# A ConvNeXt block and a selective scan on one core: the first convolution's last 16 channels by halves of the images, the norm of the first half beside the second half's products, and the parameters loaded and used beside the convolution

## The chip, the cores and the metric

The kernel runs on one core of a Trainium2 chip. The time is the device time of one execution in microseconds, the median of several runs. Beside it there is one profiled execution, from which all durations are taken.

## What is computed

The input x has 32 images of 96 channels, 56 x 56, in float32. Two layers follow each other:

```python
# layer 0
h = conv_general_dilated(x, conv_w, padding 3, feature_group_count=C) + conv_b   # 7x7, depthwise
h = transpose(h, (0, 2, 3, 1))
mu, var = mean(h, axis=-1), var(h, axis=-1)              # over the 96 channels
h = (h - mu) * rsqrt(var + LN_EPS) * ln_g + ln_b
h = gelu(einsum('bhwc,cf->bhwf', h, w1) + b1)            # 96 -> 384, exact gelu
h = einsum('bhwf,fc->bhwc', h, w2) + b2                  # 384 -> 96
x = transpose(h, (0, 3, 1, 2)) * layer_scale + x
# layer 1
x = silu(conv_general_dilated(x, conv_w, padding 2, feature_group_count=C) + conv_b)  # 5x5, depthwise
# then a selective scan over the 3136 positions with N = 4 states per channel
```

The norm of a position needs all 96 channels of the convolution at that position: this is what separates the first convolution, which works channel by channel, from the MLP, which works on rows of the image with all channels.

## The kernel before, in words

There are four stages, and each hands its result to the next through a tensor in DRAM: conv1_d (first convolution), block_d (MLP), conv2_d (second convolution), and the output.

**Preparation (lines 86 to 228).** column() and across() and the lines to 131 load all parameters on SP's queue, ahead of the kernel taps of the first convolution (line 148). The taps are padded (pad, lines 149 to 156) and stored to taps1_d (157), from which the convolution reads them as Toeplitz matrices; the second convolution's taps go to taps2_d likewise (159 to 174). Lines 177 to 228 make the MLP's and the scan's weights: three groups of products (182, 190, 207), twelve copies from PSUM (185), and small operations on VectorE.

**First convolution (251 to 316).** The images are two halves (B2 = 2) of 16. The loop `for c in range(C)` takes one channel at a time: toeplitz() (234) loads the taps as two matrices into one of three buffers wts; two DMAs (272) load the channel's images of both halves into xt, 56 rows on the partitions each; POOL (281), VectorE (278) and ScalarE (279, 282) copy the odd and the even columns to xq, one of three buffers; eight products (286, each two records in the trace) go to a pair of PSUM banks; ScalarE evicts them with the bias (294) to ht, which POOL stores to conv1_d (298). The statistics run along: VectorE sums the difference to channel 0 (302, 303), ScalarE squares it (304), VectorE sums the squares (305). After the last channel lines 308 to 314 turn the sums of all 112 rows into reciprocal standard deviations, which SP stores to rstd_d (316).

**MLP (322 to 435).** The 112 rows (two halves of the images by 56) are taken in 28 groups of RB = 4, each in two half groups k. load_rows(n) issues on SP one load of r from rstd_d (345), three of h from conv1_d (350), one for each block of 32 channels with the four rows slowest, and twelve of x (355). normalise (362, VectorE), hidden (372 on TensorE, Gelu on ScalarE 382) and result (391 on TensorE, 402 on VectorE) follow. The tiles o, r, h, x and g are all in one pool, mlp, which lies on the memory that the first convolution's pools have left.

Then the second convolution and the scan, which are not changed.

**What sets the order.** A planner orders each engine's instructions ahead of time, by the order of the program and by when it expects operands to be ready; each engine then works through its own list in that order. pin (keep_in_program_order) puts an instruction behind the one written before it on its engine. normalise, hidden and the products of result are pinned, the loads of load_rows, the convolution and the preparation are not. A pool's `bufs` says how many tiles of one kind are there at once, and a new tile waits until the old one in its place has been used.

Of the kernel before, what the change touches and what calls it, by code (L numbers as in the profile page):

```python
# [38 lines left out]
EPS = 1e-9  # L39
RB = 4  # L40
# [6 lines left out]
def convnext_then_scan_kernel(  # L47
# [38 lines left out]
    def column(src, n, name):  # L86
        t = const.tile([n, 1], F32, name=name)
        nc.sync.dma_start(t, src.rearrange("(p o) -> p o", o=1))
        return t

    def across(src, parts, n, name):
        t = const.tile([parts, n], F32, name=name)
        nc.sync.dma_start(t, src.rearrange("(o n) -> o n", o=1).to_broadcast([parts, n]))
        return t
# [9 lines left out]

    c1b_t = across(c1b, ROWS, C, "c1b_t")
    c2b_t = across(c2b, 128, C, "c2b_t")
    g_t = column(ln_g, C, "g_t")
    lnb_t = column(ln_b, C, "lnb_t")
    b2_t = column(b2, C, "b2_t")
    ls_t = column(ls, C, "ls_t")  # L110
    ls_b = across(ls, 128, C, "ls_b")
    dtb_t = column(dtb, C, "dtb_t")
    ds_t = column(ds, C, "ds_t")
    w1_t = const.tile([C, F], F32, name="w1_t")
    nc.sync.dma_start(w1_t, w1)
    b1_t = const.tile([128, 3], F32, name="b1_t")
    nc.sync.dma_start(b1_t, b1.rearrange("(f p) -> p f", p=128))
    w2_t = const.tile([128, 3, C], F32, name="w2_t")
    nc.sync.dma_start(w2_t, w2.rearrange("(f p) c -> p f c", p=128))
    xp_t = const.tile([R, C], F32, name="xp_t")  # L120
    nc.sync.dma_start(xp_t, xp[:R, :])
    xpT_t = const.tile([C, R + 2 * N], F32, name="xpT_t")
    nc.sync.dma_start(xpT_t, xpT)
    dtwT_t = const.tile([R, C], F32, name="dtwT_t")
    nc.sync.dma_start(dtwT_t, dtwT)
    a_t = const.tile([128, NG], F32, name="a_t")
    for g in range(NG):
        nc.sync.dma_start(
            a_t[:, g : g + 1],
            bass.AP(alog.tensor, alog.offset + g * DG, [[1, DG], [C, N], [1, 1]]),  # L130
        )

    w1r_t = const.tile([128, C // CB, F], F32, name="w1r_t")
    b1p_t = const.tile([128, 3], F32, name="b1p_t")
    b2r_t = const.tile([128, C // CB], F32, name="b2r_t")
    wd_t = const.tile([C, C], F32, name="wd_t")
# [5 lines left out]
    with tc.tile_pool(name="prep", bufs=1) as prep, tc.tile_pool(  # L142
        name="prep_ps", bufs=1, space=PSUM
    ) as prep_ps:


        kt = prep.tile([C, K1, K1], F32, name="kt1")
        nc.sync.dma_start(kt, c1w.rearrange("c (i j) -> c i j", j=K1))
# [3 lines left out]
        for i in range(3):  # L152
            for t in range(P1):
                j = 2 * t + 1 - i
                if j in range(K1):
                    nc.vector.tensor_copy(pad[:, i, at : at + K1, t], kt[:, :, j])
        nc.sync.dma_start(taps1_d, pad.rearrange("c d p t -> c (d p t)"))

        kt = prep.tile([C, K2, K2], F32, name="kt2")
        nc.sync.dma_start(kt, c2w.rearrange("c (i j) -> c i j", j=K2))  # L160
        turned = prep.tile([C, K2, K2], F32, name="turned")
        for r in range(K2):
            nc.vector.tensor_copy(turned[:, r], kt[:, K2 - 1 - r])
        pad = prep.tile([C, QC, 2 * RW, QC * 2], F32, name="pad2")
        nc.vector.memset(pad, 0.0)
        for k in range(QC):
            for f in range(QC):
                for t in range(2):
                    j = 4 * t + (k if k < 2 else k - 4) - f + K2 // 2
                    if j in range(K2):  # L170
                        nc.vector.tensor_copy(
                            pad[:, k, RW - K2 : RW, f * 2 + t], turned[:, :, j]
                        )
        nc.sync.dma_start(taps2_d, pad)
# [76 lines left out]
    with tc.tile_pool(name="c1", bufs=3) as pool, tc.tile_pool(  # L251
# [4 lines left out]
        for t in wts + xqs:  # L256
            nc.vector.memset(t, 0.0)
# [544 lines left out]
```

## Time and profile before

| | |
|---|---|
| time, median of 3 runs | 3655.25 us (3648.51 to 3655.76) |
| profiled execution: its own time | 3655.9 us |
| profiled execution: span, first to last instruction | 3654.1 us |
| mean granted TensorE clock | 0.827 |
| busy: PE, VectorE (DVE), ScalarE (ACT), GpSimd (POOL) | 3060.6, 2655.5, 2341.0, 1950.5 us |
| first convolution: first product, last product ends | 27.9, 609.8 us |
| MLP: first product, last product ends | 644.3, 1496.0 us |
| second convolution: first product | 1506.5 us |

Lines of the profile name an engine, a line of the kernel, and what is written from what. PE is TensorE's products, PEld its weight loads, SPq the queue of SyncE, which issues DMAs. A bracket gives the idle time of the engine before the instruction and what ended it. Buffer numbers are left out of the names: ps is any ps tile, w_t is w1_t or w2_t. The share of DMA is the mean over the core's 16 DMA engines; the granted clock is a share of full speed.

### The profile page before, as it was taken

How to read it: one execution, taken by the hardware profiler on the slowest of the kernel's cores; microseconds unless marked ns; L12 is line 12 of the kernel's file. 1: busy time of each engine (PE TensorE's matmuls, PEld its weight loads, DVE VectorE, ACT ScalarE, POOL GpSimd, SP SyncE). 2: the span in 40 equal slices, each digit the busy share in tenths (PEclk: the TensorE clock that was granted, in tenths of full speed). 3: DMA queues.
4: the chain of work that ended last, by engine and by line, in shares of the span. 5: the costliest groups of instructions: out<-in, count | busy, mean ns of one | idle time of the engine just before them, and what ended most of it. 6: DMA issues, size and time to landing. Idle time of an engine off the chain costs nothing. (4 is left out here: it accounts for less than half of the span.)

```text
span 3654.1 us, 46458 instructions
## 1 busy us (share of the span) xinstructions
PE 3060.6 (84%) x17290; PEld 1286.4 (35%) x17290; DVE 2655.5 (73%) x1771; ACT 2341.0 (64%) x2133; POOL 1950.5 (53%) x1241
## 2 busy tenths in 40 slices
PE   7999996899999999899957777777777777777775
PEld 5777774333333333333312222222222222222221
DVE  5666665233333333599949999999999999999998
ACT  3555553333333333577858878888888888888884
POOL 2333332122222222100028999999999999999996
PEclk9999998899999999999966666666666666666666
DMA  5555553455555554699977778877877877878873
GB/s 153 166 167 167 168 168 107 149 162 160 163 163 162 162 160 125 169 281 281 288 232 264 259 253 281 276 257 267 276 260 267 281 245 275 274 244 277 281 258 108
DMA packets 302054, 790.70 MB, mean 216 GB/s; under 512 B 123012, under 2 KB 180164, under 8 KB 277156
## 3 DMA queue, kind: packets, MB, share of 16 engines
q1 hardware_dynamic: 259076, 669.31, 56.7%
q0 software_dynamic: 28416, 79.87, 7.3%
q10 hardware_dynamic: 14336, 38.54, 2.7%
q8 instruction: 137, 2.24, 0.3%
q14 instruction: 89, 0.73, 0.1%
HBM read 551.83 MB, written 235.74 MB: 216 GB/s over the span
## 5 line engine op out<-in xcount | busy, mean ns | idle before, releaser
L682 POOL TENSOR_TENSOR hs<-hs,ct 128x1568 f32<-128x1568 f32 x192 | 673.3, 3507 | 104.8 <-DVE hs L671 93.0
L664 DVE TENSOR_TENSOR_SCAN pv<-rep,pv 128x1568 f32<-128x1568 f32 x192 | 664.5, 3461 | 72.2 <-ACT rep L650 54.2
L654 POOL TENSOR_TENSOR rep<-rep,bt 128x1568 f32<-128x1568 f32 x192 | 674.9, 3515 | 14.6 <-DMA rep<-du_d 14.6
L382 ACT ACTIVATE g<-ph,b1p_t 128x896 f32<-128x896 f32 x336 | 320.5, 1005 | 511.8 <-PE ph L372 511.8
L402 DVE SCALAR_TENSOR_TENSOR o<-po,b2r_t,x 128x224 f32<-128x224 f32 x336 | 190.4, 608 | 572.4 <-PE po L391 572.4
L286 PE MATMUL ps<-xq,wt 120*112 120x448 f32 x1536 | 581.9, 540 | 14.1 <-POOL xq L281 14.1
L414 POOL DMA_DIRECT2D block_d<-o x336 | 183.7, 553 | 703.5 <-DVE o L402 621.3
L286 PEld LDWEIGHTS ps<-xq,wt 120*112 120x112 f32 x1536 | 429.4, 280 | 166.2 <-POOL xq L281 14.3
L372 PE MATMUL ph<-h,w1r_t 32*128 32x448 f32 x4032 | 440.3, 559 | 55.8 <-DVE h L362 54.4
L599 POOL TENSOR_TENSOR du<-du,xs 96x784 f32<-96x784 f32 x128 | 236.3, 1847 | 373.7 <-ACT du L593 373.7
L585 PE MATMUL pz<-xs,wd_t 96*96 96x392 f32 x512 | 277.3, 707 | 172.0 <-ACT du L593 139.1
L391 PE MATMUL po<-g,w_t 128*32 128x448 f32 x4032 | 413.1, 543 | 0.0
L695 PE MATMUL py<-hs,sel_t 128*32 128x392 f32 x1536 | 328.6, 685 | 68.5 <-POOL hs L682 68.5
L630 PE MATMUL pk<-bn,pick_t 8*128 8x392 f32 x1024 | 287.3, 682 | 98.4 <-ACT y L705 78.8
L667 DVE SCALAR_TENSOR_TENSOR pv<-pv,rep 128x1568 f32<-128x1568 f32 x192 | 345.6, 1800 | 21.1 <-POOL hs L682 1.4
L480 PE MATMUL ps<-xq,wt 128*32 128x448 f32 x3072 | 309.9, 548 | 39.3 <-DMA xq<-block_d 36.5
L671 DVE TENSOR_TENSOR_SCAN hs<-rep,carry_h,pv 128x1568 f32<-128x1568 f32 x96 | 334.0, 3479 | 10.4 <-DVE pv L667 0.5
L503 DVE COPY st<-yt 28x896 f32<-28x896 f32 x288 | 317.7, 1103 | 26.9 <-DMA conv_d<-st 13.2
L671 DVE TENSOR_TENSOR_SCAN hs<-rep,pv 128x1568 f32<-128x1568 f32 x96 | 328.4, 3421 | 10.3 <-DVE pv L667 0.9
L688 PE MATMUL py<-xs,dsm_t 96*96 96x392 f32 x512 | 308.6, 746 | 11.7 <-ACT bn L618 6.1
L648 ACT ACTIVATE rep<-rep,a_t 128x1568 f32<-128x1568 f32 x192 | 308.3, 1606 | 11.6 <-DMA rep<-du_d 11.2
L649 ACT ACTIVATE rep<-rep,lift_t 128x1568 f32<-128x1568 f32 x192 | 307.6, 1602 | 6.2
(85 smaller groups left out, 3155.4 us busy)
## 6 DMA issues: line engine op xcount, KB each, us to landing
rep<-du_d SPq DMA_DIRECT2D x192, 1568.0 KB
du_d<-du SPq DMA_DIRECT2D x128, 588.0 KB
xq<-block_d SPq DMA_DIRECT2D x192, 225.0 KB
block_d<-o POOLq DMA_DIRECT2D x336, 120.0 KB, 5.6
xt<-in_x_dram SPq DMA_DIRECT2D x192, 196.0 KB
h<-conv_d SPq DMA_DIRECT2D x84, 448.0 KB
x<-in_x_dram SPq DMA_DIRECT2D x336, 112.0 KB
conv_d<-st SPq DMA_DIRECT2D x96, 392.0 KB
```

Of the source, the lines that this page charges most:

```text
L286: nc.tensor.matmul(ps[:, j, :PQ].rearrange("p (i r) -> p i r", i=BI), lhsT=wv[:KR, t], rhs=xq[:KR, j, :, t : t + W2], start=(t == 0), stop ...
L372: pin(nc.tensor.matmul(phs[i // 2][:, i % 2, :HALF], lhsT=w1r_t[rows, d, f * 128 : (f + 1) * 128], rhs=hts[n, d][rows, s * HALF : (s + 1) ...
L382: nc.scalar.activation(gt, ph[:, :, :HALF], AF.Gelu, bias=b1p_t[:, f : f + 1], scale=1.0)
L391: pin(nc.tensor.matmul(po[CB * i : CB * i + CB, :HALF], lhsT=w2_t[:, f, CB * d : CB * d + CB], rhs=gts[n, s, f, i // 2][:, i % 2], start=( ...
L480: pin(nc.tensor.matmul(ps[RW * f : RW * f + RW, h, : B * QW].rearrange("p (b q) -> p b q", q=QW), lhsT=wv[:, f, t], rhs=xv[:, :, t : t + Q ...
L503: pin(copy(st[:, :, :, :, f], yt[RW * f : RW * f + QR].rearrange("p h (b q) -> p h b q", q=QW),))
L654: pin(nc.gpsimd.tensor_mul(ut, ut, bts[i // NG]))
L664: pin(nc.vector.tensor_tensor_scan(grown, da, zero, pv[:, last : last + 1] if q else 1.0 / EPS, ALU.mult, ALU.add))
L667: pin(nc.vector.scalar_tensor_tensor(run, in0=grown, scalar=1.0, in1=ut, op0=ALU.min, op1=ALU.mult))
L671: pin(nc.vector.tensor_tensor_scan(ht, da, run, carry_h[:, col : col + 1] if q else 0.0, ALU.mult, ALU.add))
L682: pin(nc.gpsimd.tensor_mul(ht, ht, cts[k]))
L695: pin(nc.tensor.matmul(py[g * DG : (g + 1) * DG, s, :BK], lhsT=sel_t, rhs=hss[k * NG + g][:, cols], start=False, stop=True, tile_position= ...
```

## The change

The parameters are loaded on ScalarE's queue, and SP begins with the taps and the images of two channels. The weights of the MLP and the scan and the second convolution's taps are made in 13 pieces (beside), one behind each job from the fourth on, and their products use the convolution's PSUM tiles. The convolution's loop runs over jobs: 80 channels with both halves of the images, then 16 channels with the first half alone, then the same 16 with the second half. Taps are loaded four jobs ahead into five buffers, images two jobs ahead. The norm is computed by halves of the images (finish_norm): the first after the second job of the second half (job 97), the second inside the MLP at k == 3. Its store goes from SP to POOL's queue. The MLP's pool is split in three: o and g (14 buffers instead of 15) lie below, on the convolution's memory, and r, h and x above them. Some memsets go from VectorE to POOL, among them those of o.

```diff
+APART = 16
...
-    def column(src, n, name):
-        t = const.tile([n, 1], F32, name=name)
-        nc.sync.dma_start(t, src.rearrange("(p o) -> p o", o=1))
-        return t
...
+    front = ctx.enter_context(ExitStack())
+    stats = front.enter_context(tc.tile_pool(name="stats", bufs=1))
+    first = stats.tile([ROWS, B2, HALF], F32, name="first")
+    acc1 = stats.tile([ROWS, B2, HALF], F32, name="acc1")
+    acc2 = stats.tile([ROWS, B2, HALF], F32, name="acc2")
+    sq = stats.tile([ROWS, B2, HALF], F32, name="sq")
+
+    def finish_norm(j):
+
+        a1, a2 = acc1[:, j], acc2[:, j]
+        nc.vector.tensor_mul(sq[:, j], a1, a1)
+        nc.vector.scalar_tensor_tensor(
+            a2, in0=sq[:, j], scalar=-1.0 / C, in1=a2, op0=ALU.mult, op1=ALU.add
+        )
+        nc.vector.tensor_scalar(a2, a2, 1.0 / C, 0.0, ALU.mult, ALU.max)
+        nc.scalar.activation(a2, a2, AF.Sqrt, bias=eps_t[:ROWS], scale=1.0)
+        nc.vector.reciprocal(a1, a2)
+        for s in range(2):
+            nc.gpsimd.dma_start(
+                rstd_d[j * H : (j + 1) * H, s * PQ : (s + 1) * PQ], a1[s * H : (s + 1) * H]
+            )
+
+    with tc.tile_pool(name="c1", bufs=3) as pool, tc.tile_pool(
+        name="c1k", bufs=1
+    ) as keep, tc.tile_pool(name="prep", bufs=1) as prep, tc.tile_pool(
+        name="c1_ps", bufs=4, space=PSUM
+    ) as psum:
+        wts = [keep.tile([128, 2, H * P1], F32, name=f"wt1_{i}") for i in range(5)]
+        xqs = [keep.tile([128, B2, BI, W2 + 3], F32, name=f"xq_{i}") for i in range(3)]
+        jobs = [(c, (0, B2)) for c in range(C - APART)]
+        jobs += [(c, (j, j + 1)) for j in range(B2) for c in range(C - APART, C)]
...
+        kt1 = prep.tile([C, K1, K1], F32, name="kt1")
+        nc.sync.dma_start(kt1, c1w.rearrange("c (i j) -> c i j", j=K1))
+        xts: dict = {}
+
+        def load_x(n):
+            c, js = jobs[n]
+            xts[n] = pool.tile([128, COLS], F32, name=f"xt1_{n}", tag="xt")
+            for j in range(*js):
+                nc.sync.dma_start(xts[n][MP * j : MP * j + H], x[c, j * H : (j + 1) * H])
+
+        for n in range(2):
+            load_x(n)
+
+        def column(src, n, name, pool=prep):
+            t = pool.tile([n, 1], F32, name=name)
+            nc.scalar.dma_start(t, src.rearrange("(p o) -> p o", o=1))
+            return t
...
+        c1b_t = across(c1b, ROWS, C, "c1b_t", const)
...
         nc.sync.dma_start(taps1_d, pad.rearrange("c d p t -> c (d p t)"))
+        for t in wts + xqs + [acc1, acc2]:
+            nc.vector.memset(t, 0.0)
+
+        c2b_t = across(c2b, 128, C, "c2b_t", const)
+        dtb_t = column(dtb, C, "dtb_t", const)
+        g_t = column(ln_g, C, "g_t")
...
+        w1_t = prep.tile([C, F], F32, name="w1_t")
+        nc.scalar.dma_start(w1_t, w1)
...
+        def bank(name):
+            return psum.tile([128, B2, 512], F32, name=name, tag="ps")
...
+        def first_weights():
+
+            cen = prep.tile([C, C], F32, name="cen")
+            nc.vector.tensor_scalar(cen, ident[:C, :C], -1.0 / C, None, ALU.add)
+            nc.vector.tensor_scalar(w1g, w1_t, g_t, None, ALU.mult)
+            held["w1"] = bank("ps_w1")[:, 0]
+            nc.tensor.matmul(held["w1"][:C, :F], lhsT=cen, rhs=w1g, start=True, stop=True)
+            ps = bank("ps_b1")[:, 0]
...
+        def first_rows(i):
+            for d in range(C // CB):
+                nc.vector.tensor_copy(
+                    w1r_t[CB * i : CB * i + CB, d, :], held["w1"][CB * d : CB * d + CB, :F]
+                )
...
+        beside = [first_weights] + [lambda i=i: first_rows(i) for i in range(RB)]
+        beside += [second_weights, scan_weights, scan_rows, turn_taps]
+        beside += [lambda k=k: second_taps(k) for k in range(QC)]
+
+        def taps_of(n):
+
+            c, wt = jobs[n][0], wts[n % len(wts)]
+            for s in range(2):
...
+                nc.sync.dma_start(wt[MP * s : MP * s + H], taps)
+
+        for n in range(4):
+            taps_of(n)
+        for n, (c, js) in enumerate(jobs):
+            if n + 4 < len(jobs):
+                taps_of(n + 4)
+            if n + 2 < len(jobs):
+                load_x(n + 2)
+
+            xq, xt = xqs[n % len(xqs)], xts.pop(n)
+            for j in range(*js):
                 xv = xt[MP * j : MP * j + H].rearrange("p (i r s) -> p s i r", i=BI, s=2)
...
+                copy = nc.vector.tensor_copy if j else nc.gpsimd.tensor_copy
+                copy(xq[:H, j, :, 2 : W2 + 2], xv[:, 1])
+                nc.scalar.copy(xq[MP:KR, j, :, 1 : W2 + 1], xv[:, 0])
...
+            half = slice(*js)
+            ht = pool.tile([ROWS, B2, HALF], F32, name=f"ht_{n}", tag="ht") if c else first
             nc.scalar.activation(
-                two(ht), ps[:, :, :PQ], AF.Identity, bias=c1b_t[:, c : c + 1], scale=1.0
+                ht[:, half], ps[:, half], AF.Identity, bias=c1b_t[:, c : c + 1], scale=1.0
             )
...
+                nc.vector.tensor_sub(dt[:, half], ht[:, half], first[:, half])
+                nc.vector.tensor_add(acc1[:, half], acc1[:, half], dt[:, half])
+                nc.scalar.activation(dt[:, half], dt[:, half], AF.Square)
+                nc.vector.tensor_add(acc2[:, half], acc2[:, half], dt[:, half])
+            if n >= 3 and beside:
+                beside.pop(0)()
+            if n == C + 1:
+                finish_norm(0)
...
-    with tc.tile_pool(name="mlp", bufs=2) as pool, tc.tile_pool(
+    with tc.tile_pool(name="mlp_ot", bufs=1) as pool_o, tc.tile_pool(
+        name="mlp_g", bufs=14
+    ) as pool_g, tc.tile_pool(name="mlp", bufs=2) as pool, tc.tile_pool(
...
         for t in ots:
-            nc.vector.memset(t, 0.0)
+            nc.gpsimd.memset(t, 0.0)
...
-                gt = pool.tile([128, 2, HALF], F32, name=f"g_{n}_{s}_{f}_{a}", tag="g", bufs=15)
+                gt = pool_g.tile([128, 2, HALF], F32, name=f"g_{n}_{s}_{f}_{a}", tag="g")
...
+            if k == 3:
+                finish_norm(1)
...
+    front.close()
```

## Prediction

> **What bounds the kernel now.** I read the span and clock first, then the busy shares by stretch, then the timeline and the waits around the two places that the change touches: the start and the seam between first convolution and MLP. By stretch (columns: stretch, its length, busy microseconds of PE, PEld, DVE, ACT, POOL with instruction counts, granted clock, DMA share, GB/s):
>
> ```profile
> 0.00:60.00 60.00, 35.70 (x88) 24.33 (x89) 34.75 (x103) 16.75 (x23) 10.16 (x24) 1.00 0.53 146
> 300.00:360.00 60.00, 60.00 (x161) 44.51 (x160) 36.67 (x40) 31.40 (x41) 18.59 (x30) 1.00 0.54 167
> 1620.00:3654.00 2034.00, 1540.40 (x6660) 506.85 (x6651) 1892.03 (x775) 1624.47 (x1347) 1586.88 (x608) 0.70 0.78 260
> ```
>
> The first convolution is bound by PE (60.00 of 60; DVE, ACT and POOL have room), the scan, which is not changed, by DVE. The waits of the first 60 us (columns: us in total, times, longest):
>
> ```profile
> POOL xq L281 <- DMA xt<-in_x_dram: 29.9, 3, 25.9
> ...
> PE ps L286 <- POOL xq L281: 14.1, 1, 14.1
> ```
>
> and of the seam, 600 to 660:
>
> ```profile
> PE ph L372 <- DVE h L362: 39.8, 3, 34.4
> ...
> DVE h L362 <- DMA h<-conv_d: 15.3, 3, 8.2
> ```
>
> At the start PE has nothing of the convolution until the images come; in the timeline its first product stands at 27.90. At the seam PE is idle for 34.4 us in one piece:
>
> ```profile
> 609.94 1.01 ACT L294 ACTIVATE ht<-ps,c1b_t 112x896 f32<-112x896 f32 x1 [1.73 <-PE ps L286]
> ...
> 619.59 5.75 DVE L314 RECIPROCAL acc<-acc 112x896 f32<-112x896 f32 x1 [2.45 <-ACT acc L313]
> 625.37 0.75 SPq L316 DMA_DIRECT2D rstd_d<-acc  x2
> 628.58 0.62 SPq L345 DMA_DIRECT2D r<-rstd_d  x1
> 628.85 0.86 DVE L335 MEMSET o<- 128x960 f32 x1 [3.50 <-DMA rstd_d<-acc]
> 629.25 3.16 SPq L350 DMA_DIRECT2D h<-conv_d  x3
> ...
> 642.97 1.09 DVE L362 TENSOR_TENSOR h<-h,r 128x896 f32<-128x896 f32 x1 [8.23 <-DMA h<-conv_d]
> 644.27 1.88 PE L372 MATMUL ph<-h,w1r_t 32*128 32x448 f32 x8 [34.42 <-DVE h L362]
> 647.48 1.09 DVE L362 TENSOR_TENSOR h<-h,r 128x896 f32<-128x896 f32 x1 [3.42 <-DMA h<-conv_d]
> 652.22 1.09 DVE L362 TENSOR_TENSOR h<-h,r 128x896 f32<-128x896 f32 x1 [3.64 <-DMA h<-conv_d]
> ```
>
> It is a chain: last statistics and norm (609.9 to 625.3), store and reload of the norm (to 628.6 and on), then three loads of h that land 4.5 us apart. Behind it PE restarts at half clock. The whole price: the MLP ends at 1496.0 (last L391 product); its normalisations recur every 29.98 us, so its 56 half groups need 56 x 14.99 = 839.5, and it starts in effect at 656.5. The convolution's products end at 609.8, so the seam costs **46.7 us**.
>
> Last, the order in which SP issues (end of the convolution):
>
> ```profile
> 575.46 0.76 SPq L272 DMA_DIRECT2D xt<-in_x_dram  x2
> 579.73 12.81 SPq L242 DMA_DIRECT2D wt<-taps_d  x6
> ```
>
> The last channel's images are issued ahead of the taps of three channels: a load that isn't pinned goes out as soon as it can, not in program order. And the first memset of o waits for the store of acc, a tile of the pool that its own pool lies on: a pool waits for what was beneath it.
>
> **What the Trainium skill says.** DMA: Bandwidth & Descriptors, section on why a DMA increments its semaphore by 16: a DMA runs on the largest number of engines up to 16 that divides the slowest dimension on both sides. The loads of r and h have four rows there, so 4 of 16; the trace agrees (DMA share 0.24 in 630 to 635, and 448 KB in 4.5 to 4.7 us). Same page, queues and rings: each queue's descriptors are taken in ring order, so an image load behind such loads waits on those four engines; the trace has the h loads one after another, but not yet such a mix. TensorE: Matmul & The Clock Gate, Part 1: an idle window of about 3.4 us halves the clock; the trace has 0.50 from 615 to 660 and 1.00 from 665. ScalarE: Activation LUTs, on the cost of a table load: about 1283 ns; the trace has 1.28 us.
>
> **The change, part by part.** The sum is made against the profiled execution, 3655.9 us (span 3654.1 and 1.8 around it); the median shown, 3655.25, is 0.65 lower.
>
> *Start.* SP's 21 parameter DMAs before the first kernel taps (0.47 us apart, so taps only at 10.45) go away; taps and two channels of images come first. Taps issued at 0.74 land about 2.5 us later (an issue to landing of 2.2 to 4.4 us is seen at 8.5 to 12.1 and 3.1 to 7.5), ten copies to pad take 0.83: 4.2. The store of the taps to its first reload took 20.77 - 17.11 = 3.7: 8.0. Reload, as image loads in before (24.28 to 27.22), 2.9 with its issue, two of them 0.38 apart: 11.3. ACT now issues 19 DMAs ahead of its first copies: 0.32 each (L706, its only DMA row) to 0.47 (SP's spacing) gives 6 to 9 us, then probably a table load of 1.28 and a copy of 0.59: 8.6 to 11.5. So 11.3 to 11.5, if nothing comes between. But the MLP's r, h and x tiles now sit in a pool beyond everything that the convolution uses, so the 36 x loads for which there are buffers (9 tiles of 4) depend on nothing and may float into SP's idle time here: 0.42 us each, from none to 36 x 0.42 = 15 us. I take three: **first product at 12.5**, a gain of 27.9 - 12.5 = **-15.4** (0 to -16.6).
>
> *Parameter work beside the products.* PE gets 2 + 6 + 2 records (L182, L190, L207: 3.66 us at the start, where the array was cold); warm, **+2.3** (1.8 to 3.7), now on the path. DVE gets about 14 us (12 copies L185 of 0.56, 20 of L171 of 0.08, the rest small) over 13 jobs, at most 1.7 in one; it is busy 36.67 of 60, 3.7 a channel of 6.03, so 2.3 are free: nothing, and without that cover up to 14. The weight tile holds one of four PSUM pairs for some jobs; eviction takes 1.01 us, so two would do. Memsets moved to POOL aren't in the trace there (128x128 takes 0.20, DVE 0.86 for 128x960): 0.9 to 1.5 each, six of them, not before the first result needs them: nothing, at worst a few us.
>
> *Halves.* 16 channels become 32 jobs of half the products, 3.01 us each: PE's sum is unchanged. Per job, taps are loaded anew: 2 x 98 + 196 KB in, 196 out, in 3.01 us, or 200 GB/s against 167 (share about 0.65). SP needs 3 issues, 1.2 us; DVE half of three 1.09 and a copy of 0.39, 2.1; ACT about 1.7; POOL at most 0.58 + 1.28. All fit in 3.01. Images are issued some 4.5 jobs ahead (575.46 against a first product at 603): 13.5 us of lead in halves, some 10 after landing and copy. Into this come the norm of half one (half of 1.09 + 1.09 + 0.63 + 1.04 + 5.75, a table load, so 6.1 us) and up to nine h loads and three r loads. The wait for Sqrt holds ACT's evictions and copies behind it, the store of the norm now holds POOL's convolution stores: each by some us, against three output buffers (9 us). Most h loads (channels below 64) can go out long before, where the lead is 27 us; three h and three r in the halves are 6 x 4.6 = 28 us of the four engines, not all at once. I take **+3** (0 to 46, see the rivals).
>
> *Seam.* Norm of half one is done some 25 us before the products end: job 97's statistics about 10 us into the second half of 48, then 6.1 + queueing and a store of 3.6. So r and h can be there. What is late next: DVE's tail of the last job, since the first normalisation is pinned behind it: eviction 0.57, two half operations 1.1, Square 0.5, one more 0.55, about 3.1; three normalisations of 1.09 make 6.4; the third block's products start there. In before that point (653.36) lay 3.1 ahead of the effective start; with 4 instead of 34 idle us I take 2.5: 9 us. If the last h load is behind stores or SP's last taps, 12 to 15. I take **12 instead of 46.7: -34.7** (9 to 24).
>
> *Second norm inside the MLP.* 4.4 us of DVE and up to two table loads (2.6), where PE is the limit (29.76 of 30.30) and ACT 11.4, DVE 10 of 30.3: hidden by three PSUM pairs, **+1** (0 to 4). 14 instead of 15 g tiles: twelve are live at most: 0.
>
> Sum: -15.4 + 2.3 + 3 - 34.7 + 1 = -43.8; 3655.9 - 43.8 = 3612.1, so **3612**.
>
> **Rivals.** (A) *The h loads wait for the last convolution store anyway* (one tensor, conv1_d, is written in all jobs). Then they go out at 0.6 + 3.6 = 4.2 after the products, land at 4.2 + 2.5 + 3 x 4.6 = 20.5, effective start 24: **3624**. For it: h waited in before. Against: in the scan, stores to du_d follow 0.05 us after loads of other parts of it, without waiting. (B) *The x loads float ahead of the taps*: 15 us at the start, **3627**. For it: 575.46 above. Against: SP is idle there for some us only. (C) *Slower*: nine h and three r loads pile up on four engines in front of the second half's images. Each takes 4.6 us alone; if convolution traffic stretches them to 7, 84 us less 10 of lead is a stall of 74, and the seam then takes 9: 3655.9 - 15.4 + 2.3 + 74 + 9 - 46.7 + 1 = **3680**. It decides from a stall of 46.7 - 9 + 15.4 - 2.3 - 1 = 50, that is from 5 us a load ((50 + 10) / 12) with all twelve together. Against: most can go out earlier, and r only late.
>
> **How the numbers follow.** Forecast 0.58, its own range 3600 to 3620 (best: start at 11.3, no stall, seam 9); A 0.18; B 0.12; a stall as in C, but only of some 40 us, near 3650, 0.04; C 0.08. The range of 8 in 10 takes in A and B and one short stall: 3600 to 3638. About 0.2%, 7.3 us, is what a measurement of this kernel can tell from no change. Faster 0.88 (forecast, A, B), same 0.04, slower 0.08.
>
> **What would show it.** Right: the first convolution product at 11 to 14; the stretch of products with no gap except around the parameters; r and h issued on SP before the last products; the third normalisation within 12 us of the last product; clock at 0.5 for no more than some us; the scan unchanged in length. Wrong: the first product beyond 18 (B); h issued after the last store (A); PE waiting for xq or xt in the halves, with DMA share near a quarter (C).

## The result, and the profile after it

| | before | after |
|---|---|---|
| median of 4 runs each, us | 3654.06 | **3616.1** |
| lowest to highest | 3648.51 to 3655.76 | 3614.36 to 3618.94 |
| profiled execution: time / span | 3655.9 / 3654.1 | 3618.94 / 3617.1 |
| mean granted clock there | 0.827 | 0.831 |

The ratio after / before is **0.9899**, with a 95% interval of 0.9885 to 0.9912: about 38 us, or 1.0%, faster. The prediction was 3612.

The same view by stretch as before the change (stretch, its length, busy us of PE, PEld, DVE, ACT, POOL, granted clock, DMA share, GB/s), the last row being the second convolution and the scan, whose code is the same:

```profile
0.00:60.00 60.00, 42.11 (x110) 29.79 (x111) 40.28 (x106) 22.11 (x30) 15.30 (x32) 1.00 0.62 179
300.00:360.00 60.00, 60.00 (x160) 44.51 (x160) 36.65 (x40) 31.59 (x40) 18.38 (x30) 1.00 0.54 168
...
573.00:583.00 10.00, 7.65 (x21) 5.25 (x20) 3.04 (x6) 2.29 (x4) 1.65 (x4) 1.00 0.47 151
...
604.00:614.00 10.00, 2.15 (x14) 0.95 (x16) 8.41 (x13) 2.77 (x5) 2.85 (x6) 0.79 0.38 148
...
1584.00:3617.00 2033.00, 1533.68 (x6648) 507.00 (x6640) 1890.48 (x774) 1624.57 (x1346) 1586.11 (x608) 0.70 0.79 260
```

PE does 6.4 us more in the first 60; the middle of the convolution and the scan are as they were. Of the seam, where PE stood for 34.42 us in before, 7.85 us are left in the row from 604. New is a hole in the row from 573: PE 7.65 of 10 in the middle of the half jobs.

The first product of the convolution in the kernel before:

```profile
27.90 32.36 PE L286 MATMUL ps<-xq,wt 120*112 120x448 f32 x78 [14.10 <-POOL xq L281]
```

Timeline of PE in the kernel after: the first products, the parameter products among them, the end of the convolution and the first product of the MLP.

```profile
17.89 26.72 PE L334 MATMUL ps<-xq,wt 120*112 120x448 f32 x64 [17.89 <-DMA wt<-taps_d]
44.45 0.81 PE L247 MATMUL ps_w<-w1g,cen 96*96 96x384 f32 x2
...
579.70 24.77 PE L334 MATMUL ps<-xq,wt 120*112 120x448 f32 x64 [2.35 <-ACT xq L329]
612.32 5.38 PE L421 MATMUL ph<-h,w1r_t 32*128 32x448 f32 x28 [7.85 <-DVE h L411]
```

The convolution now starts at 17.89 instead of 27.90, has one gap of 2.35 us, ends at 604.47 (579.70 + 24.77), and the MLP's first product follows after 7.85 us instead of 34.42.

To add the parts up, I use the prediction's own measure: the MLP needs 56 x 14.99 = 839.5 us, so its **effective start** is its last product (1457.46 here) less 839.5, which is 618.0; the **seam** is that less the end of the convolution, 618.0 - 604.5 = 13.5. Five terms then make up the span:

| term, us | before | after | difference | predicted |
|---|---|---|---|---|
| first product of the convolution | 27.9 | 17.9 | -10.0 | -15.4 |
| first to last product of the convolution | 582.0 | 586.6 | +4.6 | +2.3 + 3 |
| seam | 46.7 | 13.5 | -33.2 | -34.7 |
| last product of the MLP to the first of the second convolution | 10.5 | 12.0 | +1.5 | 0 |
| from there to the end | 2147.6 | 2147.6 | 0.0 | 0 |

(The MLP's 839.5 is a constant of this measure; the term +1 for the second norm inside it is in the seam, and none of it is seen.) The differences sum to -37.1, the spans differ by -37.0; the terms predicted sum to -43.8. The 4 us between the predicted 3612 and the median of 3616.1 flatter the prediction a little: the execution that the terms are taken from took 3618.94.

One warning on reading the experiments: the last term is the same code in all kernels, but from run to run it came out between 2137.3 and 2147.6; that it is equal before and after is chance. Differences of less than some 10 us between two versions are therefore read from the terms ahead of it, not from the totals, and where an expected total was missed the text says so but rests nothing on it.

### The profile page after: what moved, and what is told of

It is laid out like the page before. It is cut to its first block, busy times and chain, and to the rows that moved or that the text cites. A ratio compares the mean times of both kernels' runs of the same rounds, so it can differ in the third digit from the quotient of the medians.

```text
span 3617.1 us, 46656 instructions
## 1 busy us (share of the span) xinstructions
PE 3051.3 (84%) x17290; PEld 1285.1 (36%) x17290; DVE 2659.5 (74%) x1816; ACT 2347.6 (65%) x2166; POOL 1973.9 (55%) x1286
## 5 line engine op out<-in xcount | busy, mean ns | idle before, releaser
L334 PE MATMUL ps<-xq,wt 120*112 120x448 f32 x1536 | 582.9, 540 | 20.2 <-DMA wt<-taps_d 17.9
L334 PEld LDWEIGHTS ps<-xq,wt 120*112 120x112 f32 x1536 | 428.7, 280 | 172.7 <-issue 20.2
L701 ACT ACTIVATE rep<-rep,a_t 128x1568 f32<-128x1568 f32 x192 | 308.4, 1606 | 13.5 <-DMA rep<-du_d 13.1
L702 ACT ACTIVATE rep<-rep,lift_t 128x1568 f32<-128x1568 f32 x192 | 307.7, 1602 | 6.2
L703 ACT ACTIVATE rep<-rep,lift_t 128x1568 f32<-128x1568 f32 x192 | 307.6, 1602 | 6.3
```

What stands on the lines that cost most here:

```text
L334: nc.tensor.matmul(ps[:, j].rearrange("p (i r) -> p i r", i=BI), lhsT=wv[:KR, t], rhs=xq[:KR, j, :, t : t + W2], start=(t == 0), stop=(t = ...
```

## The experiments

None of these kernels leaves out any of the computation. All are edits of the kernel after, unless said. "Ratio" is to the kernel before, run on the same chip beside it. The terms come from each kernel's own trace:

| kernel | first product | convolution | seam | second convolution begins at | median | ratio, 95% |
|---|---|---|---|---|---|---|
| before | 27.9 | 582.0 | 46.7 | 1506.5 | 3654.06 | 1 |
| after | 17.9 | 586.6 | 13.5 | 1469.5 | 3616.1 | 0.9899 [0.9885, 0.9912] |
| no_halves | 17.8 | 584.0 | 51.9 | 1503.2 | 3647.89 | 0.9991 [0.9985, 0.9998] |
| no_halves_r_first | 17.4 | 584.2 | 30.5 | 1481.4 | 3626.49 | 0.9928 [0.9915, 0.9942] |
| one_pool | 18.0 | 582.8 | 34.0 | 1487.0 | 3626.96 | 0.9929 [0.9915, 0.9944] |
| params_late | 12.1 | 585.9 | 13.7 | 1463.6 | 3606.48 | 0.9879 [0.9862, 0.9895] |
| norm_free | 18.2 | 590.2 | 13.7 | 1473.9 | 3617.38 | 0.9906 [0.9892, 0.9921] |
| h_by_rows | 17.2 | 583.4 | 10.6 | 1464.0 | 3605.58 | 0.9875 [0.9861, 0.9888] |
| square_late | 17.0 | 597.8 | 10.5 | 1477.1 | 3620.82 | 0.9918 [0.9904, 0.9931] |
| half_8 | 17.1 | 583.7 | 17.7 | 1468.0 | 3614.67 | 0.9898 [0.9884, 0.9911] |
| late_rows | 12.1 | 584.1 | 10.6 | 1459.1 | 3603.81 | 0.9866 [0.9853, 0.988] |
| late_rows_square | 11.9 | 583.7 | 10.5 | 1458.7 | 3601.43 | 0.9862 [0.9848, 0.9875] |
| late_rows_8 | 11.8 | 584.3 | 10.3 | 1456.0 | **3596.9** | 0.9849 [0.9836, 0.9863] |

### What the seam is made of: the halves, the pools, the order

**no_halves** keeps the new start and the new pools, and takes the halves back:

```diff
-APART = 16
+APART = 0
...
-            if n == C + 1:
-                finish_norm(0)
+        for j in range(B2):
+            finish_norm(j)
...
-            if k == 3:
-                finish_norm(1)
```

> All 96 channels with both halves of the images, both norms computed after the last channel; early parameters, split pools and everything else as in the changed kernel. Theory (the seam shrinks for two reasons of about the same size: the norm of one half is ready before the products end, and the loads of h and x no longer wait for the convolution's memory): the norm is on the path again, some 12 us to the first half's reciprocal, 3 to store it, 7 for r to land, while h is already there; effective start of the MLP 26 to 30 us after the last product (46.7 before, 13.5 changed), no stall in the halves; time 3627 to 3632. Rival 1 (the early loads alone do it): seam 14 to 18, time 3616. Rival 2 (the norm's halves alone do it): seam 44 to 47, time 3645 to 3649.

Measured: 3647.89, ratio 0.9991. The 10 us won at the start are there; 5.2 are lost again at the seam, 51.9 instead of 46.7, and 2.0 in the convolution, which now holds the parameter products. The theory's time was missed by 16 us. The time is the one that rival 2 gave, but not for its reason: the seam is longer than in any of the three. Its trace at the seam, DVE, PE and SP (for SP, the second number is how long it took over the issues):

```profile
607.32 19.11 SPq L399 DMA_DIRECT2D h<-conv_d  x7
626.56 24.75 SPq L394 DMA_DIRECT2D r<-rstd_d  x4
...
647.69 3.09 DVE L411 TENSOR_TENSOR h<-h,r 128x896 f32<-128x896 f32 x3 [30.39 <-DMA r<-rstd_d]
...
648.93 6.20 PE L421 MATMUL ph<-h,w1r_t 32*128 32x448 f32 x28 [47.09 <-DVE h L411]
```

With pools of their own, the h tiles have room at once, and the loads of h need only the convolution's stores: seven of them, 448 KB each on four DMA engines, go out at 607.32, ahead of r, which needs the norm and is issued at 626.56. All three normalisations then wait for that one r until 647.69; from 626 to 646 the DMA share is 0.25, four engines of 16. Here an early load was an advantage only for the load that was needed first.

**no_halves_r_first** tests that reading. It is no_halves with the h loads from the second group on held in program order, so that they can't pass r:

```diff
-                nc.sync.dma_start(ht, rows_of(conv1_d, row, d))
+                ins = nc.sync.dma_start(ht, rows_of(conv1_d, row, d))
+                if n:
+                    pin(ins)
```

> The kernel without halves (both norms after the last channel), with the h loads of every group but the first kept behind r of their group in SyncE's order. Theory (without halves seven h loads, ready as soon as the convolution is stored, go out ahead of r and take 4.6 us each one after another, so that r lands 35 us late): r goes out at about 618, lands 5 to 8 us later, effective start of the MLP 25 to 32 us after the last product instead of 51.9; time 3624 to 3631. Rival (the norm chain itself, store and reload, takes that long without halves): seam 45 to 52, time 3643 to 3648.

Measured: seam 30.5, ratio 0.9928. The two kernels differ in nothing but the order of issue, and differ by 21.4 us at the seam. In the SP queue r now stands ahead of the pile:

```profile
607.07 0.54 SPq L399 DMA_DIRECT2D h<-conv_d  x1
617.33 1.05 SPq L394 DMA_DIRECT2D r<-rstd_d  x2
618.42 3.47 SPq L399 DMA_DIRECT2D h<-conv_d  x3
```

**one_pool** is the opposite: halves as in the change, but o, g, r, h and x in one pool again, as in before:

```diff
-    with tc.tile_pool(name="mlp_ot", bufs=1) as pool_o, tc.tile_pool(
-        name="mlp_g", bufs=14
-    ) as pool_g, tc.tile_pool(name="mlp", bufs=2) as pool, tc.tile_pool(
+    with tc.tile_pool(name="mlp", bufs=2) as pool, tc.tile_pool(
...
-                gt = pool_g.tile([128, 2, HALF], F32, name=f"g_{n}_{s}_{f}_{a}", tag="g")
+                gt = pool.tile([128, 2, HALF], F32, name=f"g_{n}_{s}_{f}_{a}", tag="g", bufs=14)
```

> The changed kernel with o, g, r, h and x in one pool again, which lies on the convolution's memory; halves and early norm stay. Theory (both reasons): r and three h loads start only when the convolution's last store and last statistics are through, 7 us after the last product, 4.6 us each and 2.5 of latency; effective start 28 to 34 us after the last product; the short stall of TensorE at 577 goes, since no h load runs among the halves; time 3630 to 3636. Rival 1 (the early loads alone do it): seam 44 to 47, time 3647. Rival 2 (the norm alone does it): seam 14 to 18, time 3616.

Measured: seam 34.0, no gap among the half jobs, ratio 0.9929; as the theory said, at its upper end (its time, 3630 to 3636, was too high by 3). PE and SP there:

```profile
604.83 0.66 SPq L392 DMA_DIRECT2D r<-rstd_d  x1
605.54 1.86 SPq L397 DMA_DIRECT2D h<-conv_d  x3
...
621.52 1.88 PE L419 MATMUL ph<-h,w1r_t 32*128 32x448 f32 x8 [20.76 <-DVE h L409]
```

The norm has long been stored, but r and h can't be issued before the convolution has given up the memory that they lie in: 604.83, four us after the last product (600.76), and then come a load of r and three of h one after another.

So the seam's 33.2 us belong to no part alone. From 46.7, the pools without halves give 51.9, or 30.5 if r is kept first (-16.2); the halves without the pools give 34.0 (-12.7); both together 13.5. With sixteen half channels r goes out at 593.20, and the first normalisation doesn't wait for it; whether holding the order there as well would gain anything was not tried.

### The start

**params_late**: in the change, ScalarE issues the parameter loads in one run at the start. Here all but that of c1b are issued three per job from the first job on, and the parameter work beside the products begins four jobs later.

```diff
-        c2b_t = across(c2b, 128, C, "c2b_t", const)
-        dtb_t = column(dtb, C, "dtb_t", const)
...
+        g_t = at_column(ln_g, C, "g_t")
+        w1_t = later(prep.tile([C, F], F32, name="w1_t")[:], w1)
...
-            if n >= 3 and beside:
+            for _ in range(min(3, len(waiting))):
+                pin(nc.scalar.dma_start(*waiting.pop(0)))
+            if n >= 7 and beside:
```

> The changed kernel with all parameter loads but the first convolution's bias pinned on ScalarE's queue behind the first jobs, three a job, and the weights made from the eighth job on instead of the fourth. Theory (SyncE's loads wait for parameter loads to complete, because a load may have to wait for an earlier one of any queue): those waits of about 7 us in the first 15 us go, first product of the convolution at 11 to 13.5 instead of 17.9, time 3609 to 3612. Rival (the way of the taps itself, through pad and DRAM and back, takes that long): first product at 16 to 18, time 3614 to 3617.

The wait that made me try it is in the kernel after, the waits of SP's queue over the first 60 us (us in total, times, longest):

```profile
SPq L160 <- DMA c2b_t<-in_c2b_dram: 3.9, 1, 3.9
...
SPq L160 <- DMA xp_t<-in_xp_dram: 2.7, 1, 2.7
SPq L184 <- DMA ls_t<-in_ls_dram: 0.6, 1, 0.6
```

L160 loads images, L184 stores the taps; neither uses c2b, xp or ls, which ScalarE loads for work that comes much later. Yet by this view SP stood for 3.9 + 2.7 + 0.6 = 7.2 us until those loads had landed. But SP's is not the only path that is late. ScalarE copies half of the images' columns to xq, and its part of the first channel can't begin before it has issued its 19 parameter loads:

```profile
14.98 1.28 ACT L329 ACT_TABLE_LOAD   x1 [14.98 <-DMA a_t<-in_alog_dram]
16.28 3.65 ACT L329 COPY xq<-xt 56x448 f32<-56x448 f32 x6
```

The first of these copies ends at 16.9, the second at 17.5 (six take 3.65), and the taps that PE waits for are there at 17.89. PE needs the first copy only: in h_by_rows, with the same start but taps that came sooner, its first product stands at 17.19, between the end of the first copy (16.7) and of the second (17.4). So with SP's waits alone gone, the first product would have come at about 16.9, an estimate from these figures, one us sooner. params_late takes the parameter loads out of both paths:

```profile
12.07 50.84 PE L346 MATMUL ps<-xq,wt 120*112 120x448 f32 x128 [12.07 <-DMA wt<-taps_d]
```

(L346 is L334 with twelve lines more above it.) The first product is at 12.07 instead of 17.89, as the theory said. SP stores the taps at 4.14 instead of 7.78 and reloads them at 9.18 instead of 14.64, and the waits for parameter loads are gone from its queue; ScalarE's first copy stands at 6.63 instead of 16.28. The parameter products come later, at 62.76, at the same 0.81 us. The second convolution begins 5.9 us earlier than in the kernel after (the time, 3606.48, lies below both expectations). That the place of the parameter loads was the missing part of the start is shown; what each of the two paths would cost alone was not tried, and why SP waits for another queue's loads, the trace doesn't say.

### The gap among the half jobs, and what it costs later

**h_by_rows** loads each h tile by four loads, one for each of its four groups of 32 partitions, instead of one:

```diff
-                nc.sync.dma_start(ht, rows_of(conv1_d, row, d))
+                for i in range(RB):
+                    nc.sync.dma_start(
+                        ht[CB * i : CB * i + CB], conv1_d[CB * d : CB * d + CB, row + i, :]
+                    )
```

> The changed kernel with every h load cut into four, one for each row, with 32 channels on 32 partitions, as the x loads are. Theory (an h load with its four rows slowest runs on 4 of 16 engines, and image loads behind it on the same queue wait for these four): the stall of 2.35 us among the halves goes, the convolution gets 2 to 2.5 us shorter, and h arrives in 1 to 2 us a block instead of 4.6; the seam stays, since VectorE's and ScalarE's tail sets it; time 3612 to 3614. Rival (the stall comes from the order on SyncE or from VectorE's reciprocal, not from the four engines): the stall stays at 2 us or more, or grows, since there are four times as many loads in front of the images; time 3615 to 3619.

The Trainium skill, in DMA: Bandwidth & Descriptors, in the section on why a DMA increments its semaphore by 16, says that a load runs on as many engines, up to 16, as divide the slowest dimension of both sides; that dimension has 4 rows in the old form and 32 in the new. The trace agrees: from 616 to 620 in the kernel after the DMA share is 0.25, four engines of 16. Here is the gap in the kernel after:

```profile
563.48 0.53 SPq L399 DMA_DIRECT2D h<-conv_d  x1
...
570.14 0.33 SPq L160 DMA_DIRECT2D xt<-in_x_dram  x1
571.35 6.13 SPq L314 DMA_DIRECT2D wt<-taps_d  x2
...
579.06 0.59 ACT L329 COPY xq<-xt 56x448 f32<-56x448 f32 x1 [6.41 <-DMA xt<-in_x_dram]
```

One h load goes out at 563.48; the image load issued at 570.14 is not there until 579.06, and SP takes 6.13 us over two loads of taps, since (by the waits of its queue from 555 to 600) it stands up to 5.5 us for an h load to land. ScalarE waits 6.41 us in its copy for that image, PE 2.35 us for the copy. The stretch from 573 in h_by_rows, to be held against that of the kernel after shown above:

```profile
573.00:583.00 10.00, 10.00 (x28) 7.45 (x27) 7.57 (x14) 5.11 (x9) 3.37 (x7) 1.00 0.73 216
```

PE is at 10.00 of 10, the DMA share 0.73 instead of 0.47. The convolution is 3.2 us shorter. The seam is 2.9 shorter too, which neither the theory nor its rival had expected, and so the time, 3605.58, is below both. Its tail in the kernel after:

```profile
607.90 0.62 ACT L343 ACTIVATE ht<-ps,c1b_t 112x448 f32<-112x448 f32 x1
...
611.09 3.09 DVE L411 TENSOR_TENSOR h<-h,r 128x896 f32<-128x896 f32 x3
...
615.88 2.95 DVE L135 RECIPROCAL acc<-acc 112x448 f32<-112x448 f32 x1 [0.74 <-ACT acc L134]
```

The last eviction (L343) begins at 607.90, 3.4 us after the last product (604.47); from there to the first normalisation it is 3.19. The 3.4 are what is left of a backlog, and it can be followed back. Evictions stand at 572.04 and then not before 581.41: ScalarE's copy for the late image stood ahead of the eviction of a job whose products had ended 3.01 us ahead of the gap, at 577.35 - 3.01 = 574.3. So that eviction came 7.1 late. PE's gap gave 2.35 of it back; after that the evictions come 3.06 us apart (to 602.86), hardly faster than the products of the half jobs (24.77 us for the last eight, 3.1 each, where they take 3.01 elsewhere: the weight loads wait six times for ScalarE's copy here, 1.9 us in all, and never in h_by_rows), and only when no more copies are left, 2.52 apart. In h_by_rows ScalarE has no such wait for an image, and the last eviction comes 1.4 us after the last product (601.98 and 600.57), in late_rows 0.5 (596.73 and 596.21), in late_rows_8 0.1 (596.21 and 596.12); from it to the first normalisation it is 3.19 each time. So the late image was paid twice, as a gap in the convolution and in the tail behind it. The shorter tail is 2.0 of the 2.9 us; the other 0.9 lie behind the MLP's first product, where the granted clock is back at 1.00 by 614, while in the kernel after it falls to 0.50 once more from 620 to 622.

**square_late** takes ScalarE's Square, and the sum after it, out of the loop of waits between the two engines by doing them one job late:

```diff
-                nc.scalar.activation(dt[:, half], dt[:, half], AF.Square)
-                nc.vector.tensor_add(acc2[:, half], acc2[:, half], dt[:, half])
+                square()
+                left.append((dt, half))
...
+        square()
```

> The changed kernel with each job's Square and second sum written one job later, behind the next job's eviction. Theory (ScalarE and VectorE wait for each other in every half job: eviction, subtraction, sum, Square, 3.06 us a round against 3.01 of products, so evictions and statistics lag 3.4 us behind the last product): the last eviction comes within 1.5 us of the last product, the third normalisation 3 to 4 us earlier, effective start of the MLP 9 to 11 us after the last product instead of 13.5; time 3611 to 3614. Rival (the lag comes from the stall at 577 and the reciprocal, and is not made up whatever the order): last eviction 3 us or more behind the last product, seam 13 to 14, time 3615 to 3617.

Measured: seam 10.5, as the theory had it, but the convolution got 11.2 us longer and the time with it, 3620.82:

```profile
577.47 6.03 PE L342 MATMUL ps<-xq,wt 120*112 120x448 f32 x8 [3.21 <-ACT xq L337]
587.62 27.18 PE L342 MATMUL ps<-xq,wt 120*112 120x448 f32 x64 [4.13 <-ACT xq L337]
```

Two gaps of 3.21 and 4.13 us instead of one of 2.35 are 5.0 of the 11.2. Most of the rest is the clock: behind the first gap the granted clock is 0.50 from 578 to 582, and eight products take 6.03 us instead of 3.01; behind the second it is 0.50 from 588 to 592, and the last 64 take 27.18 instead of 24.77. Behind the gap of 2.35 in the kernel after it stays at 1.00, behind one of 2.45 in norm_free it is 0.53 from 582 to 584. With h cut by rows (late_rows_square below) the gaps are gone, and then the late Square is worth nothing at the seam: 10.5 against 10.6 without it. So the loop of waits between the two engines does not set the seam once the images come in time.

**norm_free** lets the first three normalisations go before the statistics of the last jobs:

```diff
-            pin(nc.vector.tensor_mul(hts[n, d], hts[n, d], rts[n]))
+            ins = nc.vector.tensor_mul(hts[n, d], hts[n, d], rts[n])
+            if n:
+                pin(ins)
```

> The changed kernel with the three normalisations of the first group not pinned behind VectorE's last statistics, so that they may go between those of earlier jobs. Theory (what is late at the seam is VectorE's tail of statistics, 6.7 us behind the last product, not r or h): third normalisation before or near the last product, effective start of the MLP 6 to 9 us after the last product instead of 13.5, perhaps 1 to 2 us of stall where VectorE waits for r and a copy to xq stands behind it; time 3609 to 3613. Rival (r or the last h is late anyway): third normalisation 5 us or more after the last product, seam 12 to 15, time 3615 to 3618.

Measured: 3617.38, seam 13.7 and the time as the rival said, no gain, and a convolution 3.6 us longer than in the kernel after, 1.46 of it in a gap near its end (605.06): VectorE waited 2.73 us for r in a normalisation, and a copy to xq stood behind it, as the theory had allowed for. PE's first product of the MLP:

```profile
613.72 5.38 PE L423 MATMUL ph<-h,w1r_t 32*128 32x448 f32 x28 [5.32 <-ACT ht L343]
```

The normalisations were early here, and PE's first product of the MLP waited all the same, for ScalarE's last eviction out of PSUM. That eviction is later than in the kernel after (613.05, 4.6 us after the last product) by the edit itself: the normalisations went ahead of sums that ScalarE's Square waits for (4.37 us at 608.19). So the tail is not VectorE's alone: what was put ahead there held up ScalarE, and ScalarE's evictions held PE.

**half_8** parts eight channels instead of sixteen (APART = 8).

> The changed kernel with the last 8 channels by halves instead of 16. Theory (norm of half one needs some 10 us of the second half for its last statistics, 6 to 8 for itself, 4 to store and 7 to reload, about 28 in all): with 24 us of products for the second half r lands 3 to 6 us after the last product, and two h loads of the next group go out ahead of it (9 more us on the four engines): seam 20 to 26, stall among the halves gone or small; time 3622 to 3628. Rival (16 channels are more than are needed): seam 13 to 15, time 3613 to 3617.

Measured: seam 17.7, between the theory (20 to 26) and its rival (13 to 15), no gap, and a time that can't be told from the kernel after (the rival's time, not the theory's). Half two now takes 8 x 3.01 = 24 us instead of 48, and half one's norm is that much later; DVE waits 5.88 us for r, until 612.47, when its own tail has ended at 606.6. So eight half jobs are too few as long as r and h are loaded in this form.

### Together

**late_rows** has params_late and h_by_rows in one kernel.

> The two edits that helped, together: parameter loads behind the first jobs, and h loads cut by rows. Theory (they act at different places, the start and the halves with the seam, so their gains add): first product at 12, no stall among the halves, seam 10 to 12, time 3596 to 3601, ratio to before 0.984 to 0.987. Rival (without the later start the halves or the seam meet other loads and part of the gain is lost): time 3602 to 3607.

Measured: 0.9866, and a second convolution that begins 10.4 us earlier than in the kernel after, where the two alone gave 5.9 and 5.5: the two add up but for 1 us. Seam (10.6) and ratio are as the theory said; the time, 3603.81, is in the rival's range.

**late_rows_square** adds square_late's edit.

> As the one with both edits, with Square and second sum one job later. Theory (the two stalls of 3.2 and 4.1 us that the late Square met among the halves were image loads behind h on four engines, which are gone): no stall above 1 us, seam 7 to 9, time 3593 to 3599. Rival (the stalls come from the order of ScalarE's and VectorE's work with the late Square): stalls of 5 us or more in the halves remain, time 3600 to 3608.

Measured: 0.9862, no gap, as the theory said, but its seam of 7 to 9 wasn't reached, 10.5, and the time, 3601.43, is in the rival's range; it can't be told from late_rows.

**late_rows_8** is late_rows with APART = 8 and r cut by rows as well, two edits at once:

```diff
-            nc.sync.dma_start(
-                rt, bass.AP(rstd_d.tensor, rstd_d.offset + row * COLS, [[COLS, RB], [0, CB], [1, COLS]])
-            )
+            for i in range(RB):
+                nc.sync.dma_start(
+                    rt[CB * i : CB * i + CB],
+                    bass.AP(rstd_d.tensor, rstd_d.offset + (row + i) * COLS, [[0, CB], [1, COLS]]),
+                )
```

> As the one with both edits, with r also cut by rows and 8 channels by halves instead of 16. Theory (what 8 channels lacked was time for r and h on four engines): with all 16 engines r lands within 3 us of its issue, third normalisation 6 to 9 us after the last product, seam 10 to 13, time 3596 to 3602. Rival (the norm of half one itself is too late with 24 us of products): seam 16 to 19 as with 8 channels before, time 3603 to 3608.

Measured: **3596.9** (3595.55 to 3600.0), ratio 0.9849 with an interval of 0.9836 to 0.9863: the lowest median here, faster than both the kernel before and the one after; its interval overlaps those of late_rows and late_rows_square. With h and r by rows, eight half jobs are enough; the convolution ends at 596.12, the MLP's first product follows 4.52 us later, and the seam is 10.3:

```profile
600.64 5.46 PE L440 MATMUL ph<-h,w1r_t 32*128 32x448 f32 x28 [4.52 <-DVE h L430]
```

## Why the prediction held, step by step

**Start: the mis-sized term.** Predicted -15.4, measured -10.0. The step that failed is "SP's 21 parameter DMAs before the first kernel taps [...] go away": they left SP's queue, but SP went on waiting for them, now in ScalarE's, for 7.2 us. A second step failed beside it: ScalarE's 19 issues were priced at 6 to 9 us, with the first copy done by 8.6 to 11.5; they ended at 14.95, and the first copy at 16.9. Either step alone would have kept the first product at about 17 or later. The range I gave for this term (0 to -16.6) came from x loads that might float in front. They did float, but only from 47.16 on, so rival B did not happen; that the measured gain lies in the range all the same is luck. params_late shows that the rest of the working was right to about 1 us: the store of the taps at 4.14 (4.2 in the prediction), their reload at 9.18 (8.0), the first product 2.9 after that (2.9).

**Parameter work beside the products.** Predicted +2.3; the records are 0.81 (L247), 0.72 (L250) and 0.40 (L277), 1.9 in all (1.59, 1.44 and 0.63 at the start of the kernel before). The copies on DVE and the memsets on POOL cost nothing that the trace shows.

**Halves.** Predicted +3 for the images being late, measured one gap of 2.35. The mechanism is the one that I gave for rival C, loads of h on few engines ahead of images. The lead of the images was shorter than the 13.5 us that I took: the late one was issued at 570.14 for products due at 577.35, 7.2 ahead. The stall stayed small, but not quite for my reason: of the nine h loads only two went out long before (221.75 and 414.84), not most of them. Two fell among the half jobs (558.57 and 563.48), of which the second made the gap; the other five, and r, went out from 593.20 on, when the last image had been issued (591.87) and nothing of the convolution stood behind them.

**Seam.** Predicted 12, measured 13.5. Two of its inner steps were off. The tail of the last job was to take 3.1 (its parts as listed add up to 2.7 only); from the last eviction it took 3.19, but that eviction came 3.4 late, because of the backlog that the late image left. From there on the sum held: the third normalisation ends 9.7 us after the last product (611.09 + 3.09 - 604.47), for which 6.4 were predicted without the backlog, and the effective start is 3.8 behind that, where I took 2.5 and some us of margin. One part of these 3.8 is the clock: after 7.85 us without a product PE restarts at 0.50 (612 to 616), much as in the kernel before after 34. The second norm in the MLP was predicted at +1: DVE's reciprocal at 615.88 lies behind the normalisations, beside PE's products, and costs nothing.

**The sum and the rivals.** The terms missed by +5.4 at the start, +1.5 at the seam and +1.5 behind the MLP, and by -0.7 in the convolution and -1 for the second norm. A did not happen: h is issued from 221.75 on, long before the last store at 608.81. C happened as one gap of 2.35 us instead of 74.

**Not foreseen: +1.5** between the MLP and the second convolution. The last stores of the MLP on POOL have a pause in them that nothing releases:

```profile
1457.52 5.97 POOL L463 DMA_DIRECT2D block_d<-o  x11 [2.47 <-issue]
```

Such pauses come in before, too (2.28 at 750.77, 2.47 at 1019.73, 2.28 at 1270.21), 250 to 270 us apart. In the kernels with 16 halves, one fell on the last stores before the second convolution (gap 12.0 to 13.3); in those with 8 or none it did not (9.8 to 10.5). What causes the pauses I didn't try; that stays open. The 10.3 us of seam that late_rows_8 has left can be divided: 3.3 to the first normalisation; 1.2 to the first product; 2.5 because the first 28 products take 5.46 us, at a granted clock of 0.50 to 604, where 24 take 2.54 later on; 1.8 of waiting for the first Gelu, whose table load takes 1.28; 1.4 because the next 48 products take 6.49 us instead of 5.1, at 0.62 and 0.52 from 608 to 612. So the low clock behind the idle stretch is about 3.9 of what is left.

## What to carry to other kernels

When a stretch is shortened by doing two things earlier, price each without the other as well: here neither the halves nor the pools alone gave what they gave together, and loads set free to go early went out ahead of the one that was needed first. Look in the waits of the DMA queue itself, not only of the engines, for a load that waits for another that it has no data in common with. And a short wait of an engine that works in order is paid again by whatever stands behind it in its queue, until there is slack to work the backlog off. Read the granted clock beside every gap of PE: in square_late a gap of 3.21 us cost another 3 in slower products.

## What the runs showed of the hardware that I had not expected

- By the waits of its queue, SP's loads and stores stood for loads in ScalarE's queue that they share no data with: 3.9 + 2.7 + 0.6 us at the start. With these loads issued later the waits are gone, and SP's store of the taps is at 4.14 instead of 7.78.
- ScalarE took from 0.74 to 14.95 us to issue 19 small loads, 0.75 us for each; most of the issues take 0.32 to 0.51 in the trace, and the rest are pauses between them, the longest 1.7 us (from 8.80 to 10.49).
- The same h tile by four loads of 32 partitions, not one of 4 rows x 32: gap of 2.35 us to none, DMA share 0.47 to 0.73 in that stretch, although SP issues four times as many.
- A wait of 6.41 us for one image left a backlog on ScalarE that was still 3.4 us at the end, 26 us later: its evictions came 3.06 us apart where PE's products came 3.1 apart, and 2.52 only when the copies were over.
- PE gaps of 3.21 and 4.13 us were followed by a granted clock of 0.50; one of 2.45 by 0.53, one of 2.35 by none lower than 1.00.
- POOL's issue of stores in the MLP has pauses of 2.3 to 2.5 us, from 750 on 250 to 270 us apart, in the kernel before and the one after.
